# Layer-norm sums of the FFN branch: the two channel halves are added on GpSimd, and the mean and the variance take one matmul each

## The chip, the cores and the metric

The kernel runs on one core of a Trainium2 chip. A time is the device time of one execution in microseconds; the number to be compared is the median of the runs. Five engines work side by side: TensorE (PE, with its weight loads shown apart as PEld), VectorE (DVE), ScalarE (ACT), GpSimd (POOL) and SyncE (SP), which issues the DMAs. Everything is float32.

## The reference

The input x has the shape (2, 2048, 256). It is layer-normed, and two branches work on the result: a global attention (16 heads, spatial bias) and a two-layer FFN branch with local attention. The output is x + s * silu(f), with s of the first and f of the second. One layer of the FFN branch, cut to what matters here:

```python
h = shift_token(x)            # second half of the channels: one token back
...                           # local attention on h, 8 heads of 64, windows of 128
x = x + o @ wo
h = shift_token(x)
mu = h.mean(-1, keepdims=True)
var = h.var(-1, keepdims=True)
h = (h - mu) / jnp.sqrt(var + 1e-05) * lg + lb
h = h @ w1 + b1
a, g = jnp.split(h, 2, axis=-1)
x = x + (a * gelu(g)) @ w2 + b2
```

The change concerns `mu` and `var` alone: means over 256 channels, for each token.

## The kernel before

The kernel has two stages. The first (up to about 1900 us) is the global attention. The second is `ffn_branch`, and the change lies wholly in it.

In `ffn_branch` the activations stand in SBUF with channels on partitions: `xA[b]` has 128 partitions, 2 halves of the channels (k = 0, 1) and 2049 columns of tokens. The shift by one token is done by the columns that are read: half k is read from column `cc * CH + 1 - k`. A *slot* is a layer, a chunk of 512 tokens and a batch: 2 x 4 x 2 = 16 slots. A slot has four *tiles* of 128 tokens.

A mean over channels is a sum over partitions, so it is made on PE: a 128x128 matrix `mean_w` filled with 1/256 is multiplied with the 512 columns of each half, and both products are summed in one PSUM bank. The result stands in every partition. `f_mean` (line 883) does this for the mean (`pm`, line 888), VectorE subtracts it from both halves (`hc`, line 891), ScalarE squares them (`sq`, line 895). `f_var` (line 897) does the same with the squares (`pv`, line 902); ScalarE takes the root (line 905), VectorE inverts it in four pieces (line 912) and scales `hc` (lines 917, 918). `f_gate` (pg, line 937) multiplies the result with w1, `f_out` (py, line 961, or pz, line 980, in the last layer) with w2, and `residual` (line 699) adds to `xA`.

The order of the work is written out by hand. The loop goes over tiles in steps; a step issues the pieces of

```python
STEP = "T0 T1 Q S0 S1 V K F G W0 W1 G A0 A1 G".split()
```

Q, K, V project the current tile (pp, line 721). VectorE multiplies with the rotary tables (`rot`, `swp`, lines 738 to 740), ScalarE squares, GpSimd adds (line 743), and one piece later VectorE makes the norms (`rn`, line 751) and GpSimd takes a power and multiplies (lines 752, 753). T0 and T1 transpose Q and K of the tile of the step before (pt, line 765), S0 and S1 make scores and their softmax (ps, line 790; line 803 on VectorE; line 811 on ScalarE), which GpSimd normalises one piece later (`sm`, line 825; in the first eight tiles ScalarE does it, line 822). W0 and W1 transpose the weights (pw, line 838) and copy them (`pT`, lines 843, 845), A0 and A1 sum over the values (po, line 859). G is a share of the gate pieces of an earlier slot. F is the place of the extras: `a_out` (px, line 874) in a slot's second step, `f_out` of slot s-3 in the third and fourth, `f_mean` of slot s-1 at the end of the fourth, `f_var` of slot s-2 in the first step of the next. `soon(n, ...)` puts a follow-up behind n further pieces. [...] The eight PSUM banks are used in turn.

The first nine steps use another order (FIRST_STEP), which has W and A of an older tile ahead of F.

Of the kernel before, what the change touches and what calls it, by code (L numbers as in the profile page):

```python
# [11 lines left out]
F32 = mybir.dt.float32  # L12
# [6 lines left out]
P = 128  # L19
NT = N // P  # L20
CH = 512
# [19 lines left out]
def gated_recurrent_kernel(ctx: ExitStack, tc: tile.TileContext, t: dict, out: bass.AP):  # L41
# [32 lines left out]
    s_all = [s_pool.tile([P, NT, D], F32, tag=f"s{b}", name=f"s{b}") for b in range(B)]  # L74
    global_attention(tc, t, xA, s_all, s_out, ident, eps_t, x_ch, early)
    ffn_branch(tc, t, xA, s_out, weights, ident, eps_t, mean_w, vecs, b2_row, x_ch, out_ch)


# [563 lines left out]
def ffn_branch(tc, t, xA, s_out, weights, ident, eps_t, mean_w, vecs, b2_row, x_ch, out_ch):  # L642
# [7 lines left out]
    nc = tc.nc  # L650
    with ExitStack() as ctx:
        cp = ctx.enter_context(tc.tile_pool(name="ff_c", bufs=1))
        pool = ctx.enter_context(tc.tile_pool(name="ff", bufs=2))
# [9 lines left out]
        def bank(name, shape=(P, CH)):  # L663
            turn[0] += 1
            return psr.tile(list(shape), F32, tag=f"f{turn[0] % 8}", name=name)
# [4 lines left out]
        def soon(n, f):  # L670
            later.append([n, f])

        def piece(f):
            f()
            for x in later:
                x[0] -= 1
            due = [x for x in later if x[0] < 0]
            later[:] = [x for x in later if x[0] >= 0]
            for _, g in due:
                g()  # L680
# [20 lines left out]
        def release(kind, b):  # L701
            if (kind, b) in held:
                cc, h = held.pop((kind, b))
                at = (cc + 1) * CH
                nc.vector.tensor_copy(xA[b][:, 1, at : at + 1], h)


        slots = [(l, b, cc) for l in range(DEPTH) for cc in range(NCH) for b in range(B)]
# [161 lines left out]
        def a_out(s, k):  # L870
            l, b, cc = slots[s]
            ps = bank(f"px_{s}_{k}")
            for c in range(INNER // P):
                nc.tensor.matmul(
                    ps, W["o"][:, c, k * P : (k + 1) * P], oTs[s][:, c, :],
                    start=(c == 0), stop=(c == INNER // P - 1),
                )
            residual("a", b, cc, k, ps, 0.0)


        fs = {}

        def f_mean(s):
            l, b, cc = slots[s]
            hs = [xA[b][:, k, cc * CH + 1 - k : (cc + 1) * CH + 1 - k] for k in range(2)]
            pm = bank(f"pm_{s}")
            for k in range(2):
                nc.tensor.matmul(pm, mean_w, hs[k], start=(k == 0), stop=(k == 1))
            hc = pool.tile([P, 2, CH], F32, tag="hc", name=f"hc_{s}")
            for k in range(2):  # L890
                nc.vector.tensor_sub(hc[:, k, :], hs[k], pm)
            release("f", b)
            sq = pool.tile([P, 2, CH], F32, tag="sq", name=f"sq_{s}", bufs=1)
            fs[s] = {"hc": hc, "sq": sq, "u": []}
            soon(1, lambda: nc.scalar.activation(sq, hc, AF.Square))

        def f_var(s):
            l, b, cc = slots[s]
            hc, sq = fs[s]["hc"], fs[s]["sq"]
            pw = bank(f"pv_{s}")  # L900
            for k in range(2):
                nc.tensor.matmul(pw, mean_w, sq[:, k, :], start=(k == 0), stop=(k == 1))
            rs = pool.tile([P, CH], F32, tag="rs", name=f"rs_{s}", bufs=1)
            def root():
                nc.scalar.activation(rs, pw, AF.Sqrt, bias=eps_t)
                for q in range(TPC):
                    soon(2 * q + 1, lambda q=q: invert(q))
                soon(2 * TPC + 2, lambda: scale(0))
                soon(2 * TPC + 3, lambda: scale(1))

            def invert(q):
                nc.vector.reciprocal(rs[:, q * P : (q + 1) * P], rs[:, q * P : (q + 1) * P])

            def scale(k):
                c0 = 2 * NM + k
                V = vecs[:, l, :]
                nc.vector.tensor_mul(hc[:, k, :], hc[:, k, :], rs)
                nc.vector.tensor_scalar(  # L918
                    hc[:, k, :], hc[:, k, :], V[:, c0 : c0 + 1], V[:, c0 + 2 : c0 + 3], ALU.mult, ALU.add
                )  # L920
                fs[s]["ready"] = k == 1

            gates.append(root)
# [84 lines left out]
        def out_pieces(s, k):  # L1008
            return [(lambda p=p: f_out(s, k, p)) for p in range(2)]

        def gate_pieces(s):
            return [(lambda m=m, n=n: f_gate(s, m, n)) for m in range(NM) for n in (1, 0)]
# [3 lines left out]
        for n in range(len(tiles) + 4):  # L1016
            s, i = divmod(n, TPC)
            cur, pre, pre2 = (tiles[x] if 0 <= x < len(tiles) else None for x in (n, n - 1, n - 2))
            order = FIRST_STEP if n <= N_FIRST else STEP
            if n == N_FIRST + 1:  # L1020
                order = "w0 w1 T0 T1 Q a0 a1 S0 S1 V K F G W0 W1 G A0 A1 G".split()

            def have(x):
                return 0 <= x < n_slots


            xs = []
            if s == n_slots:
                if i == 1:
                    xs = [lambda: a_out(s - 1, 0), lambda: a_out(s - 1, 1)] + out_pieces(s - 3, 0)  # L1030
                    xs += [lambda: f_mean(s - 1)]
                    gq += gate_pieces(s - 2)
                elif i == 2:
                    xs = out_pieces(s - 3, 1) + [lambda: f_var(s - 1)]
                elif i == 3:
                    xs = []
                else:
                    xs = [lambda: f_var(s - 2)]
                ng = (5, 2, 5, 5)[i]
            else:  # L1040
                if i == 0 and have(s - 2):
                    xs = [lambda: f_var(s - 2)]
                if i == 1 and have(s - 1):
                    xs = [(lambda k=k: a_out(s - 1, k)) for k in range(2)]
                if i == 1 and have(s - 2):
                    gq += gate_pieces(s - 2)
                if i >= 2 and have(s - 3):
                    xs = out_pieces(s - 3, i - 2)
                if i == 3 and have(s - 1):
                    xs = xs + [lambda: f_mean(s - 1)]  # L1050
                ng = (5, 2, 3, 2)[i]
            if i == 0 and s % B == 0 and B <= s <= per_layer:
                if s == B:
                    load_scales(1)
                load_tables(1, s // B - 1)
            if n in (1, 3, 5):
                load_tables(0, (n + 1) // 2)
            if i == 0 and s == per_layer:
                load_qkv(1)

            def run(q, n=1):
                for _ in range(n):
                    if q:
                        piece(q.pop(0))

            done = 0
            for op in order:
                j = int(op[1:] or 0)
                if op[0] in "QKV":
                    if cur:  # L1070
                        piece(lambda: a_project(*cur, "QKV".index(op)))
                elif op[0] in "TSWA":
                    if pre:
                        piece(lambda: {"T": a_turn, "S": a_scores, "W": a_weights, "A": a_sums}[op[0]](*pre, j))
                elif op[0] in "wa":
                    if pre2:
                        piece(lambda: {"w": a_weights, "a": a_sums}[op[0]](*pre2, j))
                elif op == "F":
                    while xs:
                        piece(xs.pop(0))  # L1080
                    if cur and i == 0:
                        soon(2, lambda: release("a", slots[s][1]))
                    for g in gates:
                        g()
                    gates.clear()
                else:
                    parts = order.count("G")
                    run(gq, -(-ng * (done + 1) // parts) + (-ng * done // parts))
                    done += 1

            if s == per_layer and i == 1:
                load_o(1)
            if s == per_layer + 2 and i == 0:
                load_1(1)
            if s == per_layer + 2 and i == 3:
                load_2(1)
        s = n_slots + 1
# [104 lines left out]
```

## Time and profile before

| | |
|---|---|
| median of 3 runs | 3406.14 us (3406.01 to 3406.58) |
| profiled execution, its own time | 3405.59 us |
| its span, first to last instruction | 3403.8 us |
| mean granted TensorE clock | 0.987 |
| PE busy | 3325.0 us (98%) |
| DVE busy | 2314.9 us (68%) |
| ACT busy | 2092.9 us (61%) |
| POOL busy | 1105.2 us (32%) |
| pm in f_mean, pv in f_var | 64 PE records each |

The page sums what each engine was busy with; other views cut the span into stretches, list the instructions of one tile or line with the shortest, median and longest duration in ns (a/b/c), list who waited for whom (total us, times, longest), or put instructions in order of time. In a line of the timeline the first number is the start in us from the beginning of the span, the second how long the merged group lasted, x4 how many records it has, and a bracket at the end is idle time of the engine just before it and what ended it. A stretch has its bounds, its length, busy us of PE, PEld, DVE, ACT and POOL with the number of instructions, the granted clock, the share of DMA and GB/s. Matmuls are pipelined: the end of a record is modelled and overlaps the next one, so the distance from start to start tells what one costs.

### The profile page before, as it was taken

The numbers are of one execution on the slowest core, as the hardware profiler recorded it, in microseconds if no ns is written. First come the engines' busy times: TensorE is split into PE (matmuls) and PEld (weight loads), VectorE is DVE, ScalarE is ACT, GpSimd is POOL, SyncE is SP. The second block draws the span as 40 slices with busy tenths as digits, with TensorE's granted clock in tenths as the row PEclk, the third lists the DMA queues.
The fourth block names the chain that finished last, engine by engine and source line by source line (L and its number), as shares of the span: only waits on it lengthen the run. The fifth ranks groups of instructions, "written<-read, shape, count | busy, mean of one in ns | idle before, by whom it ended". The sixth has DMA issues, their size and how long they took to land. (4 is left out here: it accounts for less than half of the span.)

```text
span 3403.8 us, 55360 instructions
## 1 busy us (share of the span) xinstructions
PE 3325.0 (98%) x21280; PEld 1631.7 (48%) x21280; DVE 2314.9 (68%) x4978; ACT 2092.9 (61%) x4237; POOL 1105.2 (32%) x949
## 2 busy tenths in 40 slices
PE   6999999999999999999999799999999999999999
PEld 3444444444444444444444355555555555666565
DVE  3798889877777787787775366666666666665642
ACT  3477676667776677767677576555555555555542
POOL 2012111111111111111111455555555555655631
PEclk8899999999999999999999899999999999999999
DMA  2100000000000100000000100000000000000001
GB/s 93 51 1 6 21 1 14 14 14 14 7 18 21 46 14 1 4 10 1 1 7 7 62 9 1 7 1 7 1 25 8 1 17 25 10 19 19 20 19 49
DMA packets 39768, 56.78 MB, mean 17 GB/s; under 512 B 8830, under 2 KB 24274, under 8 KB 39506
## 3 DMA queue, kind: packets, MB, share of 16 engines
q1 hardware_dynamic: 37266, 50.88, 4.7%
q8 instruction: 168, 2.75, 0.3%
q10 hardware_dynamic: 1728, 2.12, 0.2%
q14 instruction: 94, 0.77, 0.1%
q0 software_dynamic: 512, 0.26, 0.0%
HBM read 36.45 MB, written 16.78 MB: 16 GB/s over the span
## 5 line engine op out<-in xcount | busy, mean ns | idle before, releaser
L364 DVE TENSOR_REDUCE mx<-pm 128x1 f32<-128x512 f32 x2048 | 1272.2, 682 | 357.1 <-PE ps L397 311.7
L403 ACT ACTIVATE e<-ps 128x512 f32<-128x512 f32 x2048 | 1069.7, 602 | 258.2 <-PE ps L397 179.0
L361 PE MATMUL pm<-kT,qT 32*128 32x512 f32 x4096 | 1166.2, 626 | 3.6 <-DVE mx L364 3.6
L397 PE MATMUL ps<-qa,kT 32*128 32x512 f32 x4096 | 1109.6, 625 | 14.1 <-ACT e L403 14.1
L427 POOL TENSOR_TENSOR o<-o,part 128x512 f32<-128x512 f32 x224 | 284.3, 1269 | 1449.6 <-ACT part L426 1439.3
L361 PEld LDWEIGHTS pm<-kT,qT 32*128 32x128 f32 x4096 | 486.7, 185 | 375.3 <-DVE mx L364 262.6
L397 PEld LDWEIGHTS ps<-qa,kT 32*128 32x128 f32 x4096 | 442.1, 184 | 212.1 <-ACT e L403 142.5
L416 PE MATMUL po<-e,v 128*32 128x512 f32 x4096 | 497.5, 604 | 1.7 <-DVE mx L364 1.7
L721 PE MATMUL pp<-weights,xA 128*128 128x512 f32 x768 | 361.6, 606 | 0.8 <-DVE s L471 0.8
L937 PE MATMUL pg<-hc,weights 128*128 128x512 f32 (+1 forms) x768 | 357.6, 596 | 1.1 <-DVE hc L918 1.1
L743 POOL TENSOR_TENSOR rot<-rot,swp 128x512 f32<-128x512 f32 x128 | 166.9, 1304 | 515.6 <-DVE swp L740 504.0
L416 PEld LDWEIGHTS po<-e,v 128*32 128x32 f32 x4096 | 107.7, 109 | 353.4 <-DVE mx L364 183.9
L426 ACT COPY part<-po 128x512 f32<-128x512 f32 x224 | 131.4, 586 | 225.2 <-PE po L416 224.6
L811 ACT ACTIVATE sm<-sm,wmx 128x256 f32<-128x256 f32 (+1 forms) x512 | 249.3, 488 | 5.3 <-DVE wmx L803 4.5
L742 ACT ACTIVATE sqq<-pp 128x512 f32<-128x512 f32 x128 | 76.5, 598 | 262.5 <-DVE swp L740 254.1
L752 POOL TENSOR_TENSOR rn<-rn,mhalf 128x8 f32<-128x8 f32 x128 | 210.9, 1648 | 82.3 <-DVE rn L751 77.0
L825 POOL TENSOR_TENSOR sm<-sm,wls 128x512 f32<-128x512 f32 (+1 forms) x224 | 223.1, 1028 | 12.1 <-DVE wls L817 12.1
L937 PEld LDWEIGHTS pg<-hc,weights 128*128 128x128 f32 (+1 forms) x768 | 128.4, 178 | 156.2 <-issue 139.3
L721 PEld LDWEIGHTS pp<-weights,xA 128*128 128x128 f32 x768 | 136.6, 192 | 130.8 <-issue 122.6
L803 DVE CUSTOM_DVE_ANT_0 sm<-ps,mask 128x256 f32<-128x256 f32 (+1 forms) x512 | 181.2, 409 | 1.1 <-PE ps L790 1.0
L771 DVE COPY xT<-pt 128x512 f32<-128x512 f32 x64 | 44.2, 691 | 157.6 <-PE pt L765 157.5
L946 DVE SCALAR_TENSOR_TENSOR u<-pg,vecs,gl 128x512 f32<-128x512 f32 x96 | 70.4, 733 | 114.8 <-PE pg L937 101.4
(152 smaller groups left out, 3530.3 us busy)
## 6 DMA issues: line engine op xcount, KB each, us to landing
s<-in_x_dram SPq DMA_DIRECT2D x8, 512.0 KB, 5.0
qk_wk<-stage_wk SPq DMA_DIRECT2D x16, 256.0 KB, 2.0
kT<-qk_wk SPq DMA_DIRECT2D x128, 32.0 KB, 1.8
qk_wq<-stage_wq SPq DMA_DIRECT2D x16, 256.0 KB, 2.0
qT<-qk_wq SPq DMA_DIRECT2D x128, 32.0 KB, 1.8
s_out<-s SPq DMA_DIRECT2D x8, 512.0 KB, 2.7
s<-s_out SPq DMA_DIRECT2D x16, 256.0 KB, 3.5
x<-in_x_dram SPq DMA_DIRECT2D x16, 256.0 KB, 3.4
```

Of the source, the lines that this page charges most:

```text
L361: nc.tensor.matmul(ps, qT[rows, q0 : q0 + P], kT[rows, c * CH : (c + 1) * CH], start=True, stop=True)
L364: nc.vector.tensor_reduce(mxs[n][:, i * GH + j, c : c + 1], ps, AX.X, ALU.max)
L397: nc.tensor.matmul(ps, kT[rows, kt * P : (kt + 1) * P], qas[n][rows, :], start=True, stop=True)
L403: nc.scalar.activation(e, ps, AF.Exp)
L416: nc.tensor.matmul(pos[n][j * HP : (j + 1) * HP, :], v[:, kt, (r + j) * VW : (r + j) * VW + HP], es.pop((n, kt, j)), start=(kt % 2 == 0), ...
L427: nc.gpsimd.tensor_add(os[n], os[n], part)
L721: nc.tensor.matmul(ps, xA[b][:, k, at : at + P], W["qkv"][:, k, n * INNER : (n + 1) * INNER], start=(k == 0), stop=(k == 1),)
L752: nc.gpsimd.tensor_tensor(rn, rn, mhalf, ALU.pow)
L803: nc.vector.tensor_tensor_reduce(sm[:, x, lo:], pss[r][:, x, lo:], mask[:, lo:], -1.0, 3e38, ALU.add, ALU.min, mx[:, hb, r, x : x + 1],)
L811: nc.scalar.activation(sm[:, x, lo:], sm[:, x, lo:], AF.Exp, scale=-1.0, bias=mx[:, hb, r, x : x + 1], accum_out=ls[:, hb, r, x : x + 1],)
L825: nc.gpsimd.tensor_mul(sm, sm, ls[:, hb, r, :, None].to_broadcast([P, 2, 2 * P - lo]))
L937: nc.tensor.matmul(ps[:mw], W["1"][:, k, at : at + mw], hc[:, k, :], start=(k == 0), stop=(k == 1))
```

## The change

The two halves of the channels are added on GpSimd before PE sums over the partitions. A new piece `f_add` writes half 0 + half 1 into the first half of the tile `hc`, which is allocated there; `f_mean` multiplies this once with `mean_w` and then overwrites `hc` with the centred values as before. After the Square, GpSimd adds the two halves of `sq` in place, two pieces after `f_mean`, and `f_var` multiplies that once. `f_add` of slot s-1 is called in the third step of slot s, as the first of the extras, one step ahead of `f_mean`; at the end of the last slot it is called right behind `a_out`.

```diff
+        def halves(s):
+            l, b, cc = slots[s]
+            return [xA[b][:, k, cc * CH + 1 - k : (cc + 1) * CH + 1 - k] for k in range(2)]
+
+        def f_add(s):
+            hs = halves(s)
+            hc = pool.tile([P, 2, CH], F32, tag="hc", name=f"hc_{s}")
+            nc.gpsimd.tensor_add(hc[:, 0, :], hs[0], hs[1])
+            fs[s] = {"hc": hc}
+
         def f_mean(s):
             l, b, cc = slots[s]
-            hs = [xA[b][:, k, cc * CH + 1 - k : (cc + 1) * CH + 1 - k] for k in range(2)]
+            hs = halves(s)
             pm = bank(f"pm_{s}")
-            for k in range(2):
-                nc.tensor.matmul(pm, mean_w, hs[k], start=(k == 0), stop=(k == 1))
-            hc = pool.tile([P, 2, CH], F32, tag="hc", name=f"hc_{s}")
+            nc.tensor.matmul(pm, mean_w, fs[s]["hc"][:, 0, :], start=True, stop=True)
+            hc = fs[s]["hc"]
             for k in range(2):
                 nc.vector.tensor_sub(hc[:, k, :], hs[k], pm)
...
             soon(1, lambda: nc.scalar.activation(sq, hc, AF.Square))
+            soon(2, lambda: nc.gpsimd.tensor_add(sq[:, 0, :], sq[:, 0, :], sq[:, 1, :]))
 
         def f_var(s):
...
             pw = bank(f"pv_{s}")
-            for k in range(2):
-                nc.tensor.matmul(pw, mean_w, sq[:, k, :], start=(k == 0), stop=(k == 1))
+            nc.tensor.matmul(pw, mean_w, sq[:, 0, :], start=True, stop=True)
...
                 if i == 1:
                     xs = [lambda: a_out(s - 1, 0), lambda: a_out(s - 1, 1)] + out_pieces(s - 3, 0)
-                    xs += [lambda: f_mean(s - 1)]
+                    xs = xs[:2] + [lambda: f_add(s - 1)] + xs[2:] + [lambda: f_mean(s - 1)]
...
                 if i >= 2 and have(s - 3):
                     xs = out_pieces(s - 3, i - 2)
+                if i == 2 and have(s - 1):
+                    xs = [lambda: f_add(s - 1)] + xs
                 if i == 3 and have(s - 1):
                     xs = xs + [lambda: f_mean(s - 1)]
```

## Prediction

> **What bounds the kernel now.** I read the page's busy times first, then the second half of the span (the FFN branch, where the whole change lies) as a stretch of its own, then what TensorE waited for there, then its timeline.
>
> ```profile
> PE 3325.0 (98%) x21280; PEld 1631.7 (48%) x21280; DVE 2314.9 (68%) x4978; ACT 2092.9 (61%) x4237; POOL 1105.2 (32%) x949
> ...
> 2110.00:3300.00 1190.00, 1189.12 (x6627) 684.39 (x6627) 722.53 (x1928) 661.44 (x1461) 654.15 (x550) 1.00 0.04 13
> ...
> PE pw L838 <- POOL sm L825: 0.6, 2, 0.3
> ```
>
> In the steady stretch of the FFN branch PE is busy 1189 of 1190 us at a granted clock of 1.00; DVE is idle 467 us of it and POOL 536 us. The third line is the longest of PE's two waits from 2110 us to the end of the span; with the other (0.2 us) they sum to 0.8 us. A matmul's end is modelled, so "busy" alone proves little; the distance between starts is better. It is the same wherever 512-column matmuls follow each other:
>
> ```profile
> 3316.58 1.88 PE L888 MATMUL pm<-xA,mean_w 128*128 128x512 f32 x4
> 3318.30 3.60 PE L937 MATMUL pg<-hc,weights 128*128 128x512 f32 x8
> ...
> 3328.59 1.88 PE L902 MATMUL pv<-sq,mean_w 128*128 128x512 f32 x4
> 3330.31 17.45 PE L937 MATMUL pg<-hc,weights 128*128 128x512 f32 x40
> 3347.69 3.05 PE L980 MATMUL pz<-w,u 128*128 128x256 f32 x12
> ```
>
> Forty records of pg take 3347.69 - 3330.31 = 17.38 us, 0.434 us each; four of pm take 1.72, four of pv 1.72, so 0.43 each. PE runs at its own pace, also through the tail. A PE record taken out should therefore shorten the run by its 0.43 us, unless the next wait is closer than that.
>
> **What is removed.** Each of the 16 slots loses one matmul call in f_mean and one in f_var. The rows of pm and pv at these two lines count 64 records each for 32 calls, so one call is two records: 16 x 2 = 32 records at each line, 64 in all. At 0.43 us that is 27.5 us. Ends of this price: the pm group at 2634.28 us took until 2636.10, 0.455 each with the change of tile in it, which for all 64 makes 29.1 us; 0.43 is what two records inside a group take, and the change of tile stays, so I take 27.5.
>
> **What of it is given back.** After the shorter group PE reaches its next consumer 0.86 us sooner. Whether that is a gain depends on how long the next input has been ready. In three places it is already late:
>
> ```profile
> 2039.60 2.92 PE L838 MATMUL pw<-ident,sm 128*128 128x128 f32 x16
> ...
> 2100.75 0.66 PE L838 MATMUL pw<-ident,sm 128*128 128x128 f32 x4 [0.17 <-POOL sm L825]
> ...
> 3295.14 0.66 PE L838 MATMUL pw<-ident,sm 128*128 128x128 f32 x4 [0.34 <-POOL sm L825]
> ```
>
> The first stands just behind pv of slot 0: its 16 transposes take 2.92 us where the usual group takes 1.91, because they follow ScalarE's normalising copies (L822, eight in 3.29 us from 2038.74) one by one. The second stands behind pm of slot 1 (2095.68), the third behind pv of slot 14 (3287.61); both follow the four GpSimd products L825. There the end is set by ACT or POOL and the 0.86 us comes back as waiting: 3 x 0.86 = 2.6 us. Behind pm of slot 0 (2024.31) the same pw group has little slack; I put 0.3 us there. Together 2.9 us, which leaves 24.6 us.
>
> In the steady slots the slack is enough. The tightest place is the step with f_var (POOL, then PE):
>
> ```profile
> 2652.53 4.04 POOL L825 TENSOR_TENSOR sm<-sm,wls 128x512 f32<-128x512 f32 x4
> ...
> 2651.54 1.88 PE L902 MATMUL pv<-sq,mean_w 128*128 128x512 f32 x4
> ...
> 2656.69 1.91 PE L838 MATMUL pw<-ident,sm 128*128 128x128 f32 x16
> ```
>
> The last product ends at 2656.57. The four transposes that need it start 12 x 0.109 us (1.75 from start to start for 16) into the group, at 2658.00: 1.43 us of slack, 0.57 after the change. The sums po there (first at 2661.15) need VectorE's first copy pT, which ends near 2659.9: 1.25 us, some 0.4 after the change, since the work in front of the copy on DVE (rn, u, a reciprocal) does not come sooner. Behind f_mean pw starts at 2637.82, 3.9 us after its products ended (2633.87).
>
> **What is added: 32 adds on GpSimd.** The nearest rows are POOL's other 128x512 sums: L743 has a median of 1273 ns. 32 x 1.27 = 40.7 us. Where they stand in POOL's queue decides what they cost. At the f_mean step POOL does this:
>
> ```profile
> 2633.82 1.27 POOL L743 TENSOR_TENSOR rot<-rot,swp 128x512 f32<-128x512 f32 x1
> 2635.19 1.65 POOL L752 TENSOR_TENSOR rn<-rn,mhalf 128x8 f32<-128x8 f32 x1
> 2636.92 1.04 POOL L753 TENSOR_TENSOR rot<-rot,rn 128x512 f32<-128x512 f32 x1
> 2647.62 1.27 POOL L743 TENSOR_TENSOR rot<-rot,swp 128x512 f32<-128x512 f32 x1 [9.66 <-DVE swp L740]
> ```
>
> The sum of squares is queued behind L753 (done 2637.96) and waits for ScalarE's Square, which ends at 2638.69. It runs to about 2640, inside 9.66 us in which POOL waits for VectorE anyway; its reader f_var comes at 2651.54. Cost nothing; without that gap 1.27 us per slot on the next rotation.
>
> The sum of halves is called at the head of the extras one step earlier. Its inputs were finished a step before, and its reader f_mean is a step away. It stands between the K tile's L743 and the L752 and L753 that normalise the tile, so these end 1.27 us later: at 2616.5 instead of 2615.2 in the step before the one shown. PE's transposes of that tile start at 2621.07, so 5.9 us of slack become 4.6. Cost nothing; past 5.9 us every further microsecond would reach PE. In slot 1's step of this kind, at 2085.36, the same L753 is followed by its transposes at about 2087.9: 2.5 us of slack, 1.3 after. VectorE's and ScalarE's work is the same in the same order, and no DMA moves. The program has 15 more wait instructions on PE; I cost them at nothing (they pass while a matmul streams) and, at 0.05 us for such a record in the weight-load queue, at most 0.8 us.
>
> **Two rules that speak against the change.** The Trainium skill (GPSIMD Engine Reference, 4.1 Engine selection) gives elementwise sums to VectorE, because GpSimd needs about twice the time. The rows agree on the ratio (683 ns for hc at L891 against 1273). By that rule alone the change trades 27.5 us for 40.7 and loses 13; it counts only if POOL's time is on the path, and the 9.66 us of idle in the last line above say it isn't. The second (SBUF, State Buffer, Who interferes with whom) says that a VectorE instruction with two SBUF inputs and a GpSimd instruction that reads SBUF block each other fully. The trace shows it:
>
> ```profile
> L751 DVE TENSOR_TENSOR rn<-ss,tiny x128: 166/168/1305, 1915.6 to 3273.2; 128x8 f32<-128x8 f32 x128
> ...
> L918 DVE TENSOR_SCALAR hc<-hc,vecs x32: 544/546/1377, 2058.1 to 3356.2; 128x512 f32<-128x512 f32 x32
> ...
> L743 POOL TENSOR_TENSOR rot<-rot,swp x128: 1262/1273/1585, 1913.7 to 3273.2; 128x512 f32<-128x512 f32 x128
> ```
>
> An rn of 168 ns takes up to 1305 under a POOL sum. If each sum of halves held rn for a second turn, VectorE would be 1.27 us late in 16 steps, and with 0.4 to 1.4 us of slack most of 16 x 1.27 = 20 us could come back. But at 2143.05 us an rn between two POOL instructions that follow each other (four L825, then L743) took only 0.36 us: VectorE got in between. And behind the sum of squares VectorE has u and pT, whose other input is in PSUM. I take 0.
>
> **Sum.** 27.5 - 2.9 = 24.6 us. The profiled execution took 3405.59 us (span 3403.8 and 1.8 around it): 3381.0, span 3379.2. The median of the runs, 3406.14, is 0.55 above the profiled execution, so 3381.5.
>
> **Rivals.** (A) Partly given back: the 1.43 and 1.25 us in the f_var step aren't enough, and all 14 steady slots lose f_var's 0.86 us. Against it: both margins stay positive. For it: 0.4 us is little. 24.6 - 12.0 = 12.6 us gained, 3393.5. (B) Slower: the sum of halves in front of L752. If it held POOL for more than the 5.9 us of slack plus the slot's gain of 1.7 us, so 7.6 us, the transposes of K would lose more than is won; at 10 us, 16 x 2.4 = 38 us, 3444. Against it: no L743 took more than 1.585 us, collisions included. (C) The change doesn't shorten the run: PE's pace is set by something the modelled ends hide, 3406. Against it: the even 0.43 us at groups of 4, 8 and 40.
>
> **How the numbers follow.** The forecast has 0.80, A 0.12, B 0.04, C 0.04. A measurement of this kernel can tell about 0.2%, 6.8 us, from no change. The forecast and A are both faster: 0.92; C is the same: 0.04; B slower: 0.04. The range starts at 29.1 us gained and nothing given back, 3377.0, and ends half-way into A, 3388.
>
> **What would show it.** In the profile after: PE 21216 records, 32 each for pm and pv, groups of two with 0.43 us between starts; PE waits past 2110 us still of about 1 to 2 us in all; POOL busy about 41 us more, its wait for swp shorter by about as much; the sum of halves at 1.27 us. New PE waits on sm or pT behind pv would mean A; PE waiting for rot at L765 would mean B. The prediction is wrong if VectorE's copies come later than the 0.4 us allows, or if the adds take much longer than 1.3 us.

## The result, and the profile after

The changed kernel takes 3381.9 us in the median of six runs (3378.9 to 3383.8), the kernel before 3403.7 us beside it: a ratio of 0.9936, 95% interval 0.9926 to 0.9946. A second set of runs of both gave 0.9927 (0.9911 to 0.9943), 24.9 us of 3405.0. The forecast was 3381.5 us and 24.6 us gained. The first ratio alone says 21.8 us gained (18.4 to 25.2): that the forecast level was met within 0.4 us is in part luck, because the kernel before also came out 2.4 us faster than the 3406.14 us from which the forecast started.

The profiled executions lie further apart than the medians: spans of 3403.8 and 3377.1 us, 26.7 us. The change has no part in the first stage, and there the two executions differ already: the first projection of the FFN branch (the first `pp` of line 721) starts at 1909.84 us before and at 1907.52 after. Over the twelve profiled executions of these kernels and their variants this start wandered from 1902.9 to 1914.0 us, about as far as the times of one kernel lie apart (the changed kernel took 3372.8 to 3383.8 us in its twelve runs). I therefore compare the stretch from this start to the end of the span, the *FFN stretch*: 1494.0 us before, 1469.6 after, so 24.4 us gained. Profiled a second time, the changed kernel gave 1469.6 again.

The page of the changed kernel, the busy times of PE and POOL:

```profile
PE 3297.0 (98%) x21216; PEld 1621.1 (48%) x21216; DVE 2314.4 (69%) x4978; ACT 2091.9 (62%) x4237; POOL 1142.9 (34%) x981
```

PE has 64 records and 28 us less, POOL 32 instructions and 38 us more; VectorE and ScalarE are as they were. The same stretch as before, and the longest of PE's waits from 2110 us on:

```profile
2110.00:3300.00 1190.00, 1188.68 (x6656) 689.41 (x6655) 726.15 (x1927) 665.37 (x1464) 688.63 (x579) 1.00 0.04 14
```

```profile
PE pw L838 <- POOL sm L825: 1.0, 3, 0.3
```

PE is still busy 1188.7 of 1190 us; in this stretch it only got further. The added POOL time (688.6 us busy where it was 654.2) stands in what was idle time before. PE's timeline near the end, the counterpart of the lines shown before:

```profile
3291.59 1.02 PE L897 MATMUL pm<-hc,mean_w 128*128 128x512 f32 x2
3292.45 3.60 PE L946 MATMUL pg<-hc,weights 128*128 128x512 f32 x8
...
3302.73 1.02 PE L911 MATMUL pv<-sq,mean_w 128*128 128x512 f32 x2
3303.59 17.46 PE L946 MATMUL pg<-hc,weights 128*128 128x512 f32 x40
3320.98 3.05 PE L989 MATMUL pz<-w,u 128*128 128x256 f32 x12
```

The groups of pm and pv have two records in place of four, and the next group starts 0.86 us after them where it took 1.72. The 40 records of pg still take 0.435 us each.

Set side by side start by start, the two traces fall apart by 0.86 us behind every pm from slot 2 on and behind every pv but those of slots 0 and 14, and by nothing in between that lasts. Those two groups, pm of slot 1 and most of pm of slot 0 are where the gain came back; PE's timeline shows the waits behind pv of slot 0, pm of slot 1 and pv of slot 14 (the bracket is PE's idle time):

```profile
2036.63 3.23 PE L838 MATMUL pw<-ident,sm 128*128 128x128 f32 x16 [0.62 <-ACT sm L822]
...
2097.08 0.66 PE L838 MATMUL pw<-ident,sm 128*128 128x128 f32 x4 [0.34 <-POOL sm L825]
2098.07 0.66 PE L838 MATMUL pw<-ident,sm 128*128 128x128 f32 x4 [0.34 <-POOL sm L825]
...
3268.16 0.66 PE L838 MATMUL pw<-ident,sm 128*128 128x128 f32 x4 [0.34 <-POOL sm L825]
3269.15 0.66 PE L838 MATMUL pw<-ident,sm 128*128 128x128 f32 x4 [0.34 <-POOL sm L825]
3270.15 0.65 PE L838 MATMUL pw<-ident,sm 128*128 128x128 f32 x4 [0.34 <-POOL sm L825]
```

Behind pm of slot 1 PE waited once before and waits twice now, behind pv of slot 14 it waited twice and waits three times now: it came 0.86 us sooner and the products L825 did not.

### The profile page after: what moved, and what is told of

It reads as the page before. It is cut to its first block, busy times and chain, and to the rows that moved or that the text cites. A ratio compares the mean times of both kernels' runs of the same rounds, so it can differ in the third digit from the quotient of the medians.

```text
span 3377.1 us, 55281 instructions
## 1 busy us (share of the span) xinstructions
PE 3297.0 (98%) x21216; PEld 1621.1 (48%) x21216; DVE 2314.4 (69%) x4978; ACT 2091.9 (62%) x4237; POOL 1142.9 (34%) x981
## 4 chain that ended last, share of the span: by engine, by line
PE 90%; DVE 4%; issue 3%; ACT 2%; POOL 1%; DMA 1%; POOLq 0%; SPq 0%; DVEq 0%; ACTq 0%
PE pm L361 19%; PE ps L397 15%; PE po L416 14%; PE pp L721 9%; PE pg L946 8%; PE ps L790 3%; PE po L859 3%; PE pw L838 3%; PE px L874 3%; PE py L970 3%; PE pt L765 2%; PE pz L989 2%; DVE mx L364 1%; PE pp_wk L293 1%; PE px L466 1%
## 5 line engine op out<-in xcount | busy, mean ns | idle before, releaser
L825 POOL TENSOR_TENSOR sm<-sm,wls 128x512 f32<-128x512 f32 (+1 forms) x224 | 222.8, 1026 | 10.0 <-DVE wls L817 10.0
```

The costliest lines, as they stand in the source:

```text
L825: nc.gpsimd.tensor_mul(sm, sm, ls[:, hb, r, :, None].to_broadcast([P, 2, 2 * P - lo]))
```

## The experiments

All numbers without another name are the FFN stretch of one profiled execution: 1494.0 us before, 1469.6 us with the change. A kernel for which no ratio is given ran once.

**The two halves of the change, one at a time.** First the mean alone:

```diff
-            soon(2, lambda: nc.gpsimd.tensor_add(sq[:, 0, :], sq[:, 0, :], sq[:, 1, :]))
...
-            nc.tensor.matmul(pw, mean_w, sq[:, 0, :], start=True, stop=True)
+            for k in range(2):
+                nc.tensor.matmul(pw, mean_w, sq[:, k, :], start=(k == 0), stop=(k == 1))
```

> The sum of halves and the single matmul for the mean alone; the variance takes two matmuls as before. Theory (PE's own pace, waits at single places): from the first projection to the end of the span 1494.0 us before, 1469.6 with the whole change; here 14 slots gain 0.86 us, slot 0 some 0.3, slot 1 nothing: 12.3 us, so about 1481.7. Rival (the adds cost what POOL needs): 16 x 1.27 = 20 us of it are given back, so longer than before.

Measured: 1482.3 us, 11.7 gained (12.3 expected). Slot 0's 0.3 us came back behind its pv.

Then the variance alone:

```diff
-            nc.gpsimd.tensor_add(hc[:, 0, :], hs[0], hs[1])
...
-            nc.tensor.matmul(pm, mean_w, fs[s]["hc"][:, 0, :], start=True, stop=True)
+            for k in range(2):
+                nc.tensor.matmul(pm, mean_w, hs[k], start=(k == 0), stop=(k == 1))
```

> The sum of squares and the single matmul for the variance alone. Theory: 14 of 16 slots gain 0.86 us (not 0 and 14, where PE waits for the softmax weights right behind it): 12.0 us, so about 1482.0 us from the first projection to the end. Rival (the two gains lean on the same slack, so that the second comes to less than the first): mean alone and variance alone add up to clearly more than the 24.4 us of both.

Measured: 1482.0 us, 12.0 gained. The halves add up to 23.7 us, the whole gains 24.4. Up to the last group of pg the gains are 12.0, 12.3 and 24.4 us; the rest is the time behind PE's last matmul, 8.1 us in these two executions and 7.8 before and after. The halves do not compete for one slack: each is its own 14 groups of 0.86 us, and the 0.3 us of slot 0 is the variance's.

**The adds without the gain.**

```diff
-            nc.tensor.matmul(pm, mean_w, fs[s]["hc"][:, 0, :], start=True, stop=True)
+            for k in range(2):
+                nc.tensor.matmul(pm, mean_w, hs[k], start=(k == 0), stop=(k == 1))
...
-            soon(2, lambda: nc.gpsimd.tensor_add(sq[:, 0, :], sq[:, 0, :], sq[:, 1, :]))
+            sc = pool.tile([P, CH], F32, tag="rs", name=f"sqs_{s}", bufs=1)
+            soon(2, lambda: nc.gpsimd.tensor_add(sc, sq[:, 0, :], sq[:, 1, :]))
...
-            nc.tensor.matmul(pw, mean_w, sq[:, 0, :], start=True, stop=True)
+            for k in range(2):
+                nc.tensor.matmul(pw, mean_w, sq[:, k, :], start=(k == 0), stop=(k == 1))
```

> Both adds are issued on GpSimd where the change has them, but PE takes two matmuls for mean and variance as before (the sum of squares goes to a tile that nobody reads; the sum of halves is overwritten unread). Theory: 40 us more of POOL busy and 1494.0 us from the first projection to the end, as before, within 0.5 us. Rival (POOL's time or the shared port costs): up to 20 us longer.

Measured: 1494.2 us, 0.2 more than before, with POOL 1144 us busy instead of 1105. Some 39 us of GpSimd time cost PE nothing.

**The adds on VectorE.** Both `nc.gpsimd.tensor_add` of the change become `nc.vector.tensor_add`.

> The change with both adds on VectorE in place of GpSimd, issued at the same places. Theory: VectorE has slack at both places too (0.68 us per add instead of 1.27 us), so the same 1469.6 us from the first projection to the end, within 1 us, and the same median as the change. Rival (VectorE is the tighter engine; the sum of squares waits on it for ScalarE in front of the copies that PE needs): 1 us or more lost per slot, 1480 to 1486.

Measured: 1472.4 us, ratio 0.9944 (0.9927 to 0.996), which the timing can't tell from the change. In the FFN stretch it is 2.8 us more than with the change, where at most 1 was expected. All of it was lost in slots 0 to 2; from there to the end the two traces run in step. VectorE's waits from 2000 to 2060 us name the place:

```profile
DVE sq L905 <- ACT sq L904: 3.6, 1, 3.6
```

In slot 0 VectorE stood 3.6 us in front of the sum of squares, waiting for ScalarE's Square; behind it, in the order of issue, stood the rotary products that ScalarE, and through it PE, need next. PE then waited 2.49 us for ScalarE, and behind that wait its granted clock (the third number from the end of the second line) was 0.50:

```profile
2041.95 3.59 PE L838 MATMUL pw<-ident,sm 128*128 128x128 f32 x16 [2.49 <-ACT sm L822]
...
2043.00:2046.00 3.00, 3.00 (x16) 2.57 (x15) 1.20 (x2) 2.98 (x8) 0.00 (x0) 0.50 0.00 0
```

The rival's cost per slot did not show. In the steady slots either engine has room for the adds, as nothing was lost there.

**How much room, in front of the K tile's normalising.** The sum of halves is issued four and eight times, all but one for nothing:

```diff
-            nc.gpsimd.tensor_add(hc[:, 0, :], hs[0], hs[1])
+            for _ in range(4):
+                nc.gpsimd.tensor_add(hc[:, 0, :], hs[0], hs[1])
```

> The change with the sum of halves issued four times (three times for nothing), which makes the normalising of the K tile behind it 3 x 1.23 = 3.7 us later. Theory: the trace of the changed kernel leaves 4.8 us (first layer) to 6.1 us (second) of slack at the transposes of that tile, so only slots 0 and 1 lose, about 3 us together: 1472 to 1473 us from the first projection to the end. Rival (every microsecond of POOL in front of the normalising costs): 16 x 3.7 = 59 us more.

Measured: 1472.6 us. The loss of 3.0 us is in slots 0 and 1 but for 0.4 at the end; between slot 2 and slot 15 nothing is lost.

> The same with eight sums of halves, 7 x 1.23 = 8.6 us later. Theory: past the slack, so 8 slots of the first layer lose 3.8 us each, 5 of the second 2.5 us, slots 0, 1 and 15 some 16 us together: 59 us more than with the change, 1528, so slower than the kernel before by about 35 us, with PE waiting for rot. Rival (POOL does not reach PE at all): 1470.

Measured: 1576.8 us, 107 more than with the change where 59 were expected. The sign and the place are as expected, the size is not. PE's waits from 2110 us on, and one of the places in PE's timeline:

```profile
PE pt L765 <- POOL rot L753: 52.6, 13, 4.6
PE pm L898 <- POOL hc L891: 5.5, 1, 5.5
```

```profile
2383.67 1.11 PE L765 MATMUL pt<-ident,rot 128*128 128x128 f32 x4 [4.55 <-POOL rot L753]
2384.58 3.62 PE L721 MATMUL pp<-weights,xA 128*128 128x512 f32 x4
2388.12 2.12 PE L790 MATMUL ps<-xT,xT 64*128 64x128 f32 x28
```

The 13 waits for `rot` are 52.6 us, where 8 x 3.8 + 5 x 2.5 = 43 were expected, because sums that follow each other take 1.33 us each (eight in 10.66), not 1.23. That makes the normalising 9.4 us later than with the change; less the waits of about 4.55 us in the first layer and 3.25 in the second, the slack was some 4.9 and 6.2 us, close to the 4.8 and 6.1 that had been read. The larger part is behind the wait. The four records of pp take 3.54 us from start to start, where they take 1.82 elsewhere, and the stretches say why. The last two lines are another of the 13 places:

```profile
2376.00:2381.00 5.00, 3.12 (x22) 1.70 (x18) 0.00 (x0) 1.75 (x3) 4.76 (x5) 1.00 0.02 3
2382.00:2388.00 6.00, 4.33 (x8) 1.91 (x8) 0.69 (x1) 0.00 (x0) 1.53 (x2) 0.50 0.00 0
...
2950.41 0.66 PE L765 MATMUL pt<-ident,rot 128*128 128x128 f32 x4 [3.25 <-POOL rot L753]
...
2950.00:2957.00 7.00, 6.59 (x46) 4.04 (x47) 4.76 (x17) 2.67 (x5) 4.61 (x5) 1.00 0.33 112
```

Around the wait of 4.55 us PE's granted clock fell to 0.50, and the records behind it took twice as long. The wait of 3.25 us at 2947 us left the clock at 1.00, and that stall cost 3.5 us; the other four waits of that length were followed by a clock of 0.50 and cost 4.8 to 6.3 us. So it is the clock that makes a stall dearer than its wait. On average each of the 13 stalls cost 6.2 us, 4.05 of waiting and 2.2 of slow records: 81 us; slots 0 and 1 lost 17 and the end 9. The Trainium skill (TensorE: Matmul & The Clock Gate, Why this matters for your kernels) warns of PE-idle gaps above about 3 us between bursts of matmuls. The wait of 4.55 us agrees. But 3 us is no sharp limit in these runs: the clock stayed at 1.00 behind one wait of 3.25 us, and it fell behind the 2.49 us of the run with the adds on VectorE. By the waits alone this kernel would have ended near 1545.

**How much room behind the variance.** Rival A of the prediction lived on two margins, 1.43 us before and 0.57 us after the change. One more sum of 1.23 us, for nothing, in front of the softmax products of that step fits into the first margin and not into the second:

```diff
             def normalize():
                 nc.vector.reciprocal(ls[:, hb], ls[:, hb])
+                if hb == 0 and i == TPC - 1 and s >= 2:
+                    sc = pool.tile([P, CH], F32, tag="rs", name=f"probe_{s}", bufs=1)
+                    nc.gpsimd.tensor_add(sc, xA[0][:, 0, :CH], xA[1][:, 0, :CH])
```

> The kernel before with one more 128x512 sum on GpSimd, for nothing, in front of the softmax products in the first step of slots 3 to 16, the step of the variance. Theory: the slack there is 1.43 us and 1.25 us, the sum 1.23: nothing lost, 1494.0 to 1495 from the first projection to the end. Rival (the slack read from the trace is not real): 14 x 1.2 = 17 us.

Measured: 1494.0 us, nothing lost.

> The changed kernel with the same extra sum. Theory: only 0.57 us of slack is left there, so 13 steps lose 1.23 - 0.57 = 0.66 us: 8.5 us more than the change, 1478.1 from the first projection to the end, with PE waiting for the softmax products. Rival (the change used up no slack there, because PE's group was short of nothing): 1469.6 as without the sum.

Measured: 1481.0 us, 11.4 more than with the change. PE's timeline in one of these steps, with the sum and then in the kernel before with the same sum:

```profile
2652.15 1.67 PE L841 MATMUL pw<-ident,sm 128*128 128x128 f32 x12
2654.16 0.66 PE L841 MATMUL pw<-ident,sm 128*128 128x128 f32 x4 [0.35 <-POOL sm L828]
```

```profile
2657.43 1.91 PE L841 MATMUL pw<-ident,sm 128*128 128x128 f32 x16
```

Thirteen steps lose 0.76 us each, 9.9 us; expected were 0.66 each. The same sum costs nothing in the one kernel and 0.76 us per step in the other, so the change did use up most of that margin, and left about half a microsecond (1.23 - 0.76, where 0.57 was forecast). The bracket says 0.35 us, because the modelled ends of the matmuls hide half of the wait: 12 transposes at 0.109 us would have ended at 2653.46, and the next starts 0.70 us after that.

The other 1.4 us were lost before the first extra sum, in slot 0. VectorE and POOL in this kernel at that place, then in the changed kernel:

```profile
2033.00 1.30 DVE L751 TENSOR_TENSOR rn<-ss,tiny 128x8 f32<-128x8 f32 x1
...
2033.00 1.27 POOL L743 TENSOR_TENSOR rot<-rot,swp 128x512 f32<-128x512 f32 x1
```

```profile
2029.67 0.17 DVE L751 TENSOR_TENSOR rn<-ss,tiny 128x8 f32<-128x8 f32 x1
...
2029.67 1.31 POOL L743 TENSOR_TENSOR rot<-rot,swp 128x512 f32<-128x512 f32 x1
```

The norm and GpSimd's next sum, queued behind the sum of squares, become ready at the same moment. Here the sum came first and the norm was held for 1.30 us; in the changed kernel the norm slipped in. In seven traces that have the sum of squares on GpSimd there, the sum won once. PE then waited 1.97 us for ScalarE instead of 0.62, and here too its granted clock was 0.50 behind the wait (2044 to 2047 us).

**The change once more, and a version without its small losses.**

> The changed kernel once more, with five rounds of timing. Theory: from the first projection to the end of the span 1469.6 us, or 1.1 to 1.5 us more where the norm of slot 0 (rn) loses the race for the shared port to the GpSimd sum behind the sum of squares; ratio 0.9928 (24.4 of 3406). Rival (the gain of the profiled execution was luck of the start): 1475 and more.

Measured: 1469.6 us, ratio 0.9927 (0.9911 to 0.9943).

```diff
-            soon(2, lambda: nc.gpsimd.tensor_add(sq[:, 0, :], sq[:, 0, :], sq[:, 1, :]))
+            if s:
+                soon(2, lambda: nc.gpsimd.tensor_add(sq[:, 0, :], sq[:, 0, :], sq[:, 1, :]))
...
-            nc.tensor.matmul(pw, mean_w, sq[:, 0, :], start=True, stop=True)
+            for k in range(1 if s else 2):
+                nc.tensor.matmul(pw, mean_w, sq[:, k, :], start=(k == 0), stop=(s > 0 or k == 1))
...
-                    run(gq, -(-ng * (done + 1) // parts) + (-ng * done // parts))
+                    if s == n_slots and i == 0:
+                        run(gq, (3, 1, 1)[done])
+                    else:
+                        run(gq, -(-ng * (done + 1) // parts) + (-ng * done // parts))
```

> The changed kernel with two edits: slot 0 takes its variance with two matmuls and no sum of squares (its gain came back as waiting anyway), and in the first step behind the last slot one more gate piece goes ahead of the softmax transposes that wait for GpSimd. Theory: slot 0 loses at most 0.3 us against the change and has no race for the port; PE's wait of 0.6 us for the softmax products at 3267 us and the lost 0.86 us go, about 1.2 us gained: 1468.5 to 1469 from the first projection to the end, too little for the timing to tell. Rival (the sums behind the transposes then wait for their copies as long): 1469.6 to 1470.5.

Measured: 1469.3 us, ratio 0.9927 (0.9912 to 0.9941), the same as the change: it lies between the range of the theory and that of the rival. At the end 0.65 us were gained, not 1.2: PE waits for the copies pT there instead (0.6 us in two waits), as the rival had it. Slot 0 lost 0.3. These two edits, at least, win back nothing worth having.

## Why the prediction was right

- *PE runs at its own pace in the FFN branch.* Right: a group short of two records brought 0.86 us, 28 times, and the records between kept their distances. Rival C falls.
- *27.5 us removed, at 0.43 us a record.* Right; 0.455 us (29.1) would have been too much, since the change of tile stays.
- *2.9 us given back in slots 0, 1 and 14.* Right in place: 3.1 us came back. Slot 0 kept 0.3 us of its two groups, where I had 0.6; slot 1's pm and slot 14's pv kept nothing.
- *Margins of 0.57 and 0.4 us in the step of the variance.* The first was right. The trace after has the last product of that step end at 2643.58 and its transposes start 12 x 0.109 us after 2642.86, at 2644.17: 0.59 us. The pair of runs with the extra sum shows that it is real and how close rival A was. The second was read from the wrong copy, and that nothing was lost there was luck. VectorE and PE at this place before, then after:

```profile
2659.26 1.21 DVE L845 COPY pT<-pw 128x512 f32<-128x512 f32 x2
...
2661.15 0.43 PE L859 MATMUL po<-pT,v 128*64 128x128 f32 x2
2661.57 0.59 PE L937 MATMUL pg<-hc,weights 128*42 128x512 f32 x1
```

```profile
2646.28 1.21 DVE L845 COPY pT<-pw 128x512 f32<-128x512 f32 x2
...
2647.55 0.43 PE L859 MATMUL po<-pT,v 128*64 128x128 f32 x2
2647.74 0.59 PE L946 MATMUL pg<-hc,weights 128*42 128x512 f32 x1
2648.17 1.91 PE L859 MATMUL po<-pT,v 128*64 128x128 f32 x30
```

  The first sums wait for the second of the two copies: in all 13 steady steps of the changed kernel they start 0.05 us after its end (here 2647.50), where they started 0.67 us after it before. That is less than the 0.86 us by which PE came sooner, so they come 0.24 us late against the records around them. The wait did not lengthen the run, because a record of pg was still under way on PE: it and the sums behind it keep their 0.43 us. How much later the copy could have come was not measured.
- *The adds cost nothing.* Right: 1494.2 us with the adds alone. Both stand where they were put. POOL's timeline in a changed step and in the next one:

```profile
2598.96 1.26 POOL L743 TENSOR_TENSOR rot<-rot,swp 128x512 f32<-128x512 f32 x1
2600.18 1.27 POOL L890 TENSOR_TENSOR hc<-xA 128x512 f32<-128x512 f32 x1
2601.41 1.65 POOL L752 TENSOR_TENSOR rn<-rn,mhalf 128x8 f32<-128x8 f32 x1
...
2626.14 1.27 POOL L905 TENSOR_TENSOR sq<-sq 128x512 f32<-128x512 f32 x1 [0.30 <-ACT sq L904]
2634.65 1.27 POOL L743 TENSOR_TENSOR rot<-rot,swp 128x512 f32<-128x512 f32 x1 [7.24 <-DVE swp L740]
```

  The first delays the normalising by 1.2 us inside its slack, which the runs with four and eight sums bracket. The second lies in POOL's wait for swp, which is 7.24 us where it was 9.66.
- *The rule that gives elementwise sums to VectorE* was weighed rightly: on VectorE the same adds did not gain more.
- *The shared port.* I took 0. In the steady slots that holds: no norm was held a second time. In slot 0 a race can cost some 1.4 us; I did not see that the sum of squares of slot 0 stands close in front of the next rotary sum there, since ScalarE is late in that step. The sum ought to have had 0 to 1.4 us for it.
- *Rival B.* Its mechanism is real and its threshold was right; one sum of 1.27 us is about a fifth of the 5.9 us that it takes. Its price was too low: by its rule eight sums of 10.7 us would have cost 16 x 3.1 = 50 us against the kernel before, and they cost 83, mostly because the slow clock behind the waits came on top.

The sum of 24.6 us was made against the profiled execution of before; its 3379.2 us of span came out as 3377.1 because the first stage was 2.3 us shorter in that execution. For the FFN stretch alone the forecast was 1469.4, the measurement 1469.6.

## What to carry to other kernels

Where one engine runs without a gap, work taken from it is worth its start-to-start distance, but only up to the next input that is already just in time: list those places and subtract them one by one. Before giving the work to an idle engine, look at what stands behind it in that engine's queue and how long its readers can wait; the engine's share of busy time says nothing on that. When a gain of less than 1% is to be explained, compare the stretch that the change touches, since the rest of the program may wander by as much.

## What the runs showed of the hardware

A wait on PE can cost more than its length: 13 waits of 3.2 to 4.6 us cost 2.2 us each on top, on average, with a granted clock of 0.50 behind most of them; I had priced waits at their length. The length of the wait alone did not decide it here, since the clock fell behind one of 2.49 us and held behind one of 3.25. And a wait in PE's rows can be twice as long as its bracket says: 0.35 us shown, 0.70 us from start to start.
